# Layer 1's q and k projections by seven block products instead of eight, on one core of Trainium2

## The chip, the cores and the metric

The kernel runs on one core of one Trainium2 chip. The core has five engines with queues of their own: TensorE (PE, matmuls; its weight loads are shown as PEld), VectorE (DVE), ScalarE (ACT), GpSimd (POOL) and SyncE (SP, which here issues the transfers). [...] The metric is the device time of one execution in microseconds, as a median over runs.

## The reference

The input x has the shape 1 x 128 x 256 x 256: 128 rows of 256 tokens with 256 channels. There are two layers, both in float32, and each adds its result to its input.

```python
x = x + _L0_conv_ref(_gn(x), ...)   # gated attention along a row, 8 heads, pair bias from z
x = x + _L1_conv_ref(_gn(x), w_in, b_in, w_out, b_out, 16)

def _L1_conv_ref(x, w_in, b_in, w_out, b_out, band):     # H = 4 heads, D = 64
    qkv = x2 @ w_in.T + b_in
    q, k, v = jnp.split(qkv, 3, axis=-1)
    ...
    scores = jnp.einsum('bhid,bhjd->bhij', q, k) / jnp.sqrt(D)
    keep = jnp.abs(i - j) <= band
    scores = jnp.where(keep, scores, -jnp.inf)
    attn = jax.nn.softmax(scores, axis=-1)
    out = jnp.einsum('bhij,bhjd->bhid', attn, v)
    y = out @ w_out.T + b_out
```

`_gn` is a group normalization over the whole picture with 32 groups of 8 channels. The change concerns layer 1 alone, and of it the products that give q and k.

## The kernel before, in words

A first stage reads x and z and takes the statistics of the first normalization. Layer 0 follows, and writes its result to DRAM. Then comes layer 1, in `fast_kernel` from line 1665 on. (A second version, `general_kernel`, runs only if a check at the end asks for it.)

Layer 1 works on pairs of rows, 64 of them, each an object of the class `Pair1`. The data of a pair lie transposed: channels on the partitions, in KC = 2 chunks of 128, and the two rows' 512 tokens along the free axis. The steps of a pair are methods:

- `turn`: VectorE transposes the loaded rows (`xs`) to `xT`. `centre(k)`: ScalarE subtracts the mean from chunk k (`xgT`), and after the second chunk GpSimd adds the output bias to the copy `xt` that waits for the residual. The scale of the normalization is multiplied into `w_in` once, in `norm1`.
- `project(which, m)`: TensorE makes one 128-channel chunk m of q or k for both rows, by two matmuls of 128x128 weights with 512 columns (line 1745). ScalarE copies it out with its bias (line 1749). A pair needs four such calls, eight matmuls.
- `values(r)`: four matmuls of 256 columns make v of row r (line 1760), and ScalarE copies them out (line 1764).
- `scores(r)`: small matmuls over the band's blocks (line 1774), the exponential on ScalarE (line 1782), and the band's mask on GpSimd (line 1784).
- `apply(r)`: small matmuls give the weighted values (`o_eo`) and the sums of the weights (`su_eo`), even and odd blocks in tiles of their own (line 1802).
- `combine(r)`: ScalarE copies the odd halves (lines 1812 and 1813), VectorE adds the even ones, takes the reciprocal (line 1815) and makes `oT` (lines 1814 to 1818).
- `out_row(r)`: four matmuls with `w_out` (line 1833), VectorE adds the residual (line 1837), and SP sends the pair to the output.

The main loop (line 1886) is written under `tc.manual_schedule()`: every engine gets its instructions in the order in which the program text issues them, and each engine runs its queue in that order. The tile layer adds the semaphore waits that the tiles' uses call for. A turn of the loop works on several pairs at once: it scores and applies the rows of `now`, finishes `was`, projects `nxt`, and centres `nn`:

```python
now.scores(0); was.apply(1); was.out_row(0); was.combine(1)
nxt.project("qT", 0); nxt.project("kT", 0); nxt.project("qT", 1); nn.centre(0)
now.scores(1); now.apply(0); now.combine(0); nxt.project("kT", 1)
nxt.values(0); nxt.values(1); was.out_row(1); nn.centre(1); n3.turn()
```

PSUM, the memory that matmuls write to, has eight banks of 512 float32 columns. Layer 1 divides them so: two tiles of one bank for products (`ps1_mm`, used in turn by `project`, `values` and `out_row` through `mm1`), one tile of two banks for the scores (`ps1_s`), and four tiles of one bank each for `o_eo` and `su_eo`.

Of the kernel before, what the change touches and what calls it, by code (L numbers as in the profile page):

```python
# [9 lines left out]
F32 = mybir.dt.float32  # L10
AF = mybir.ActivationFunctionType
ALU = mybir.AluOpType
# [4 lines left out]
P = 128  # L17
# [756 lines left out]
def fast_kernel(  # L774
# [889 lines left out]
    rsum1 = dram.tile([NP, H1, 2, I], F32, name="rsum1")  # L1664
    with tc.tile_pool(name="l1", bufs=2) as sb, tc.tile_pool(
        name="l1s", bufs=4
    ) as sm, tc.tile_pool(name="ps1_mm", bufs=2, space=PSUM) as ps_mm, tc.tile_pool(
        name="ps1_s", bufs=1, space=PSUM
    ) as ps_s, tc.tile_pool(name="ps1_o", bufs=1, space=PSUM) as ps_o:

        def mm1(name):
            return ps_mm.tile([P, 512], F32, name=name, tag="mm")

        nM1 = const.tile([P, KC], F32, name="nM1")

        def norm1():
# [4 lines left out]
            ps = ps_s.tile([P, 2, 512], F32, name="ps_gn", tag="s")  # L1681
# [14 lines left out]
            nc.vector.tensor_scalar_add(R1c, ps[:, 1, 2:4], 1e-5)  # L1696
            nc.gpsimd.tensor_tensor(R1c, R1c, mhalf[:, :KC], ALU.pow)
            nc.vector.tensor_scalar_mul(nM1, ps[:, 1, 0:2], -1.0)
            for n in range(3):
                for k in range(KC):  # L1700
                    at = slice(n * C, (n + 1) * C)
                    nc.vector.tensor_scalar_mul(w_in[:, k, at], w_in[:, k, at], R1c[:, k : k + 1])


        o_eo = [ps_o.tile([P, 2, I], F32, name=f"ps_o1_{n}", tag=f"o{n}") for n in range(2)]
        su_eo = [ps_o.tile([P, I], F32, name=f"ps_su1_{n}", tag=f"su{n}") for n in range(2)]
        for n in range(2):
            nc.vector.memset(o_eo[n], 0.0)
            nc.vector.memset(su_eo[n], 0.0)

        class Pair1:

# [19 lines left out]
            def centre(self, k):  # L1732
# [3 lines left out]
                if k == KC - 1:  # L1736
                    nc.gpsimd.tensor_tensor(self.xt, self.xt, bcast(bout_r, 1, 2 * NB), ALU.add)

            def project(self, which, m):
# [3 lines left out]
                ps = mm1("ps_p1")  # L1743
                for k in range(KC):
                    nc.tensor.matmul(  # L1745
                        ps, w_in[:, k, n * C + m * P : n * C + (m + 1) * P], self.xgT[:, k, :],
                        start=(k == 0), stop=(k == KC - 1),
                    )
                nc.scalar.activation(
                    getattr(self, which)[:, m, :], ps, AF.Identity, bias=bin_c[:, n * KC + m : n * KC + m + 1]  # L1750
                )

            def values(self, r):
                if r == 0:
                    self.v = sb.tile([P, 2, NB, C], F32, name="v1", tag="v")
                ps = mm1("ps_v1")
                for b in range(NB):
                    t = r * NB + b
                    for k in range(KC):
                        nc.tensor.matmul(  # L1760
                            ps[:, b * C : (b + 1) * C], self.xgT[:, k, t * P : (t + 1) * P], w_in[:, k, 2 * C : 3 * C],
                            start=(k == 0), stop=(k == KC - 1),
                        )
                nc.scalar.copy(self.v[:, r, :, :].rearrange("p b c -> p (b c)"), ps)

            def scores(self, r):

                ps = ps_s.tile([P, 2, 512], F32, name="ps_sc1", tag="s")
                at = lambda q, c, j: ps[:, q, (c * 2 + j) * W : (c * 2 + j + 1) * W]
                for c in range(KC):  # L1770
                    for k in range(NK):
# [32 lines left out]
                                )  # L1804

            def combine(self, r):

                if r == 0:
                    self.rv = sb.tile([P, 2, I], F32, name="rv1", tag="rv", bufs=3)
                rv = self.rv  # L1810
                odd = sm.tile([P, 3, I], F32, name="odd1", tag="odd", bufs=2)
                nc.scalar.copy(odd[:, 2, :], su_eo[1])
                nc.scalar.copy(odd[:, :2, :], o_eo[1])
                nc.vector.tensor_tensor(odd[:, 2, :], su_eo[0], odd[:, 2, :], ALU.add)
                nc.vector.reciprocal(rv[:, r, :], odd[:, 2, :])  # L1815
                nc.vector.tensor_tensor(odd[:, :2, :], o_eo[0], odd[:, :2, :], ALU.add)
                oT = sb.tile([P, 2, I], F32, name="oT1", tag="oT", bufs=3)
                nc.vector.tensor_tensor(oT, odd[:, :2, :], bcast(rv[:, r, :], 1, 2), ALU.mult)  # L1818
                self.oT[r] = oT
                if r == 1 and self.p < NP - LATE:  # L1820
                    nc.sync.dma_start(rsum1[self.p].rearrange("q r i -> q (r i)"), rv[0:P:DH].rearrange("q r i -> q (r i)"))
                elif r == 1 and self.p < NP - 1:
                    check(rv.rearrange("p r i -> p (r i)"), 1e-16, 1e8, sm)
                elif self.p == NP - 1:
                    check(rv[:, r, :], 1e-16, 1e8, sm)

            def out_row(self, r):
                if r == 0:
                    self.yo = sb.tile([P, 2 * NB, C], F32, name="yo", tag="yo")
                ps = mm1("ps_y1")  # L1830
                for b in range(NB):
                    for k in range(KC):
                        nc.tensor.matmul(  # L1833
                            ps[:, b * C : (b + 1) * C], self.oT[r][:, k, b * P : (b + 1) * P], w_out[:, k, :],
                            start=(k == 0), stop=(k == KC - 1),
                        )
                nc.vector.tensor_tensor(  # L1837
                    self.yo[:, r * NB : (r + 1) * NB, :], ps.rearrange("p (b c) -> p b c", b=NB),
                    self.xt[:, r * NB : (r + 1) * NB, :], ALU.add,
                )  # L1840
                s0 = 2 * self.p
# [22 lines left out]
        with tc.manual_schedule():  # L1864
            now, nxt = pair1(0), pair1(1)
            now.turn()
            nxt.turn()
            norm1()
            for k in range(KC):
                now.centre(k)  # L1870
            for m in range(KC):
                now.project("qT", m)
                now.project("kT", m)
            for r in range(2):
                now.values(r)
            for k in range(KC):
                nxt.centre(k)
        check_all(eb.rearrange("p h b i -> p (h b i)"), math.exp(-20.0), math.exp(20.0))
        mask_t = sb.tile([S, I], F32, name="mask_all", bufs=1)
        nc.sync.dma_start(mask_t, mask)  # L1880
# [3 lines left out]
        with tc.manual_schedule():  # L1884
            was = Nobody()
            for p in range(NP - 1):
# [6 lines left out]

                now.scores(0)
                was.apply(1)
                was.out_row(0)
                was.combine(1)
                nxt.project("qT", 0)
                nxt.project("kT", 0)
                nxt.project("qT", 1)  # L1900
                nn.centre(0)

                now.scores(1)
                now.apply(0)
                now.combine(0)
                nxt.project("kT", 1)
                if p < NP - 2:
                    nxt.values(0)
                    nxt.values(1)
                was.out_row(1)  # L1910
                nn.centre(1)
                n3.turn()
                if checks and p > 0:
                    checks.pop(0)()
# [20 lines left out]
        ps = mm1("ok_ps")  # L1935
        nc.tensor.matmul(ps[:, 0:1], ones, tot, start=True, stop=True)
        nc.vector.tensor_scalar(verdict, ps[0:1, 0:1], P - 0.5, None, ALU.is_lt)


@with_exitstack  # L1940
# [62 lines left out]
```

## Time and profile before

| | us |
|---|---|
| Median of three runs | 3310.61 |
| Lowest and highest | 3309.5, 3310.71 |
| The profiled execution, its own time | 3316.03 |
| Its span, first to last instruction | 3314.3 |
| Layer 1 in it: first scores to the end of the last row's addition (line 1837) | 2133.2 to 3307.8 |

The profile is of one execution. Its page gives, by engine, the busy time and the share of the span; the span in 40 slices with the busy share in tenths and TensorE's granted clock in tenths of full speed; and the chain of work that ended last, followed back from the end. The timeline lists an engine's instructions, merged where equal ones follow each other: start, duration, engine, line, operation, output and input tiles, shapes, count, and in brackets how long the engine was idle before and what ended the wait. A float32 matmul appears as two records, and their recorded durations overlap, so that the time of one is read from start to start.

### The profile page before, as it was taken

The page shows a single profiled execution, that of the slowest core. Times are in us where ns is not written, and L with a number is a line of the kernel's source. Part 1 is how long each engine was busy: PE and PEld are TensorE (multiplying, and loading weights), DVE is VectorE, ACT ScalarE, POOL GpSimd, SP SyncE. Part 2 cuts the span into 40 slices and gives each one's busy share as a digit, 9 for nine tenths or more (in the row PEclk, how much of TensorE's full clock was granted, in tenths as well). Part 3 has the DMA queues.
Part 4 walks back from the last instruction along what each step waited for, and adds up shares of the span by engine and source line. Part 5 has one row for each costly group of instructions (what it writes and reads, how often), then busy time and mean ns, then how long its engine had stood idle before and what let it go on. Part 6 is the DMA issues. An engine that isn't in the chain of part 4 may idle for free.

```text
span 3314.3 us, 80768 instructions
## 1 busy us (share of the span) xinstructions
PE 3157.9 (95%) x34656; PEld 1977.2 (60%) x34656; DVE 2121.6 (64%) x3179; ACT 1452.7 (44%) x2121; POOL 1962.8 (59%) x1375
## 2 busy tenths in 40 slices
PE   5389999999999999999999999699999999999998
PEld 3255555555555555555555555466666666666666
DVE  7955666666666666666666666466655555555566
ACT  2264444444444444444444444244444444444443
POOL 2378777777787777787887776233333333333332
PEclk8699999999999999999999999899999999999999
DMA  9951212212221222222122211533333434343431
GB/s 354 375 137 43 75 49 75 75 46 65 72 75 49 75 75 60 64 64 69 49 75 75 75 49 52 104 79 91 85 90 86 92 85 91 85 92 84 92 90 54
DMA packets 464879, 295.92 MB, mean 89 GB/s; under 512 B 312480, under 2 KB 413728, under 8 KB 463360
## 3 DMA queue, kind: packets, MB, share of 16 engines
q1 hardware_dynamic: 459440, 287.76, 31.7%
q8 instruction: 275, 4.51, 0.6%
q10 hardware_dynamic: 5072, 2.90, 0.3%
q14 instruction: 92, 0.75, 0.1%
HBM read 221.85 MB, written 68.75 MB: 88 GB/s over the span
## 4 chain that ended last, share of the span: by engine, by line
PE 91%; DVE 3%; DMA 3%; ACT 1%; POOL 1%; SPq 1%; issue 0%; ACTq 0%; POOLq 0%; DVEq 0%
PE ps_p L1296 21%; PE ps_p L1745 14%; PE ps_sc L1330 8%; PE ps_y L1833 7%; PE ps_ov L1362 7%; PE ps_v L1760 7%; PE ps_y L1417 7%; PE ps_v L1311 6%; PE ps_o L1802 3%; PE ps_su L1370 3%; PE ps_sc L1774 3%; PE ps_x L1274 2%; PE ps_su L1802 1%; DVE st L1178 1%; DVE zst L1103 1%; DMA zt<-in_z_dram 1%
## 5 line engine op out<-in xcount | busy, mean ns | idle before, releaser
L1351 POOL TENSOR_TENSOR eboth<-e 128x512 f32<-128x512 f32 x512 | 640.6, 1273 | 392.9 <-DVE e L1346 389.7
L1346 DVE TENSOR_TENSOR e<-ps_sc,eb 128x1024 f32<-128x1024 f32 x512 | 603.1, 1219 | 307.0 <-ACT ps_sc L1337 306.9
L1337 ACT ACTIVATE ps_sc<-ps_sc 128x1024 f32<-128x1024 f32 x512 | 492.8, 1006 | 509.2 <-PE ps_sc L1330 509.2
L1784 POOL TENSOR_TENSOR e<-e,bw 128x384 f32<-128x384 f32 x256 | 259.5, 1035 | 769.8 <-ACT e L1782 769.8
L1745 PE MATMUL ps_p<-xgT,w_in 128*128 128x512 f32 x1024 | 470.3, 602 | 4.5 <-issue 3.7
L1745 PEld LDWEIGHTS ps_p<-xgT,w_in 128*128 128x128 f32 x1024 | 190.1, 191 | 203.7 <-issue 174.8
L1330 PE MATMUL ps_sc<-qT,kT 32*128 32x256 f32 x4096 | 293.3, 400 | 2.1 <-ACT kT L1300 2.1
L1296 PE MATMUL ps_p<-xnT,wq 128*128 128x512 f32 x512 | 267.3, 634 | 3.5 <-POOL xnT L1283 3.1
L1833 PE MATMUL ps_y<-w_out,oT 128*128 128x256 f32 x1024 | 250.3, 388 | 2.6 <-DVE oT L1818 2.6
L1837 DVE TENSOR_TENSOR yo<-ps_y,xt 128x512 f32<-128x512 f32 x128 | 88.4, 690 | 251.9 <-PE ps_y L1833 149.7
L1362 PE MATMUL ps_ov<-e,v 128*32 128x256 f32 x4096 | 247.7, 382 | 0.0
L1417 PE MATMUL ps_y<-wo,oT 128*128 128x256 f32 x1024 | 242.1, 379 | 2.0 <-POOL oT L1407 1.2
L1417 PEld LDWEIGHTS ps_y<-wo,oT 128*128 128x128 f32 x1024 | 194.3, 190 | 82.5 <-issue 59.3
L1311 PE MATMUL ps_v<-wv,xnT 128*128 128x256 f32 x1024 | 242.2, 379 | 0.0
L1330 PEld LDWEIGHTS ps_sc<-qT,kT 32*128 32x128 f32 x4096 | 184.9, 184 | 94.4 <-issue 83.6
L1296 PE MATMUL ps_p<-xnT,wk 128*128 128x512 f32 x512 | 240.8, 592 | 0.0
L1296 PE MATMUL ps_p<-xgT,wg 128*128 128x512 f32 x512 | 236.8, 605 | 0.0
L1760 PE MATMUL ps_v<-w_in,xgT 128*128 128x256 f32 x1024 | 231.8, 379 | 0.0
L1815 DVE RECIPROCAL rv<-odd 128x256 f32<-128x256 f32 x128 | 224.4, 1753 | 4.4
L1760 PEld LDWEIGHTS ps_v<-w_in,xgT 128*128 128x128 f32 x1024 | 194.4, 190 | 53.5 <-issue 30.1
L1317 DVE TENSOR_TENSOR v<-ps_v,vb_r 128x512 f32<-128x512 f32 x128 | 88.6, 692 | 206.8 <-PE ps_v L1311 206.8
L1311 PEld LDWEIGHTS ps_v<-wv,xnT 128*128 128x128 f32 x1024 | 189.6, 190 | 50.8 <-issue 31.0
(169 smaller groups left out, 4989.9 us busy)
## 6 DMA issues: line engine op xcount, KB each, us to landing
xa<-in_x_dram SPq DMA_DIRECT2D x8, 4096.0 KB
xt<-in_x_dram SPq DMA_DIRECT2D x64, 512.0 KB
x<-xo SPq DMA_DIRECT2D x16, 2048.0 KB
xs<-x SPq DMA_DIRECT2D x256, 128.0 KB
xt<-x SPq DMA_DIRECT2D x64, 512.0 KB
rvb<-rsum SPq DMA_DIRECT2D x252, 128.0 KB
out_dram<-yo SPq DMA_DIRECT2D x63, 512.0 KB
zt<-in_z_dram SPq DMA_DIRECT2D x15, 2048.0 KB
```

The source lines that it names most:

```text
L1296: nc.tensor.matmul(ps, w[:, k, m * P : (m + 1) * P], getattr(self, src)[:, k, :], start=(k == 0), stop=(k == KC - 1),)
L1311: nc.tensor.matmul(self.ps_v[:, b * C : (b + 1) * C], self.xnT[:, k, t * P : (t + 1) * P], wv[:, k, :], start=(k == 0), stop=(k == KC - 1),)
L1330: nc.tensor.matmul(self.pss[q // 2][:, q % 2, b, :], self.kT[rs, c, r * I + b * P : r * I + (b + 1) * P], self.qT[rs, c, r * I : (r + 1) * I],
L1337: nc.scalar.activation(self.pss[a], self.pss[a], AF.Exp)
L1346: nc.vector.tensor_tensor(e, pss[a], eb[:, h : h + 2], ALU.mult)
L1351: nc.gpsimd.tensor_tensor(t, es[a][:, :, 0, :], es[a][:, :, 1, :], ALU.add)
L1362: nc.tensor.matmul(ov[q * D0 : (q + 1) * D0, c, :], self.v[:, r, b, h * D0 : (h + 1) * D0], es[q // 2][:, q % 2, b, :], start=(b == 0), st ...
L1417: nc.tensor.matmul(self.ps_y[:, b * C : (b + 1) * C], self.oT[r][:, k, b * P : (b + 1) * P], wo[:, k, :], start=(k == 0), stop=(k == KC - 1),)
L1745: nc.tensor.matmul(ps, w_in[:, k, n * C + m * P : n * C + (m + 1) * P], self.xgT[:, k, :], start=(k == 0), stop=(k == KC - 1),)
L1760: nc.tensor.matmul(ps[:, b * C : (b + 1) * C], self.xgT[:, k, t * P : (t + 1) * P], w_in[:, k, 2 * C : 3 * C], start=(k == 0), stop=(k == ...
L1784: nc.gpsimd.tensor_tensor(e[:, q], e[:, q], bcast(bw.rearrange("p b w -> p (b w)"), 1, KC), ALU.mult)
L1833: nc.tensor.matmul(ps[:, b * C : (b + 1) * C], self.oT[r][:, k, b * P : (b + 1) * P], w_out[:, k, :], start=(k == 0), stop=(k == KC - 1),)
```

## The change

Of a pair's centred data take the four blocks b[k][r] (chunk k, row r; 128x256), and of the q weights the four blocks w(m, k) of 128x128; the same for k. Strassen's form (in Winograd's arrangement) makes the four output blocks from seven products instead of eight. Its parts:

- `mix_weights`, once: four sums and differences of weight blocks on GpSimd (`wst`).
- `differences`, per pair: four differences of data blocks on GpSimd (`dT`), issued after the pair's second `centre`.
- `product(n, i)`: one matmul of 256 columns, for q (n = 0) or k (n = 1). A product goes to block x or block y of a tile of two banks; x lies in the first and y in the second. Products 1, 6, 7 and 4 go to x one after the other, each added to what is there, and ScalarE copies x out with the bias after each of them: the first three to `u`, the last to the result. Product 2 goes to y, later 5, and 3 is added to 5.
- `join(n, i)`: VectorE adds y and one part of `u` to a block of the result, after products 2, 5 and 3.

PSUM is laid out anew: one ring of two tiles of two banks each (`two1`), which the scores, the products of q, the products of k, and the values share in turn. Both rows' values lie in one such tile. The tile `su_y` of two banks holds the sums of `apply` in one half of each bank and the product of `out_row` in the other.

The turn of the loop is written anew as well: `combine` is split in three, `out_row(0)` moves behind the products 7 and the old pair's `weigh`, and all products stand in the first half of the turn.

```diff
-    ) as sm, tc.tile_pool(name="ps1_mm", bufs=2, space=PSUM) as ps_mm, tc.tile_pool(
-        name="ps1_s", bufs=1, space=PSUM
-    ) as ps_s, tc.tile_pool(name="ps1_o", bufs=1, space=PSUM) as ps_o:
+    ) as sm, tc.tile_pool(name="ps1_s", bufs=2, space=PSUM) as ps_s, tc.tile_pool(
+        name="ps1_o", bufs=1, space=PSUM
+    ) as ps_o:
...
+        def two1(name):
+            return ps_s.tile([P, 2, 512], F32, name=name, tag="s")
...
-        su_eo = [ps_o.tile([P, I], F32, name=f"ps_su1_{n}", tag=f"su{n}") for n in range(2)]
+        su_y = ps_o.tile([P, 2, 2, I], F32, name="ps_su_y1", tag="su")
+        su_eo = [su_y[:, n, 0] for n in range(2)]
...
+            def differences(self):
+                self.dT = sb.tile([P, 4, I], F32, name="dT1", tag="dT")
+                b = [[self.xgT[:, k, r * I : (r + 1) * I] for r in range(2)] for k in range(KC)]
+                t1, t2, t3, t4 = (self.dT[:, n] for n in range(4))
+                nc.gpsimd.tensor_tensor(t1, b[0][1], b[0][0], ALU.subtract)
+                nc.gpsimd.tensor_tensor(t2, b[1][1], t1, ALU.subtract)
+                nc.gpsimd.tensor_tensor(t3, b[1][1], b[0][1], ALU.subtract)
+                nc.gpsimd.tensor_tensor(t4, b[1][0], t2, ALU.subtract)
...
+            def product(self, n, i):
+                if len(self.ps) == n:
+                    self.ps.append(two1("ps_qk"))
+                x, y = self.ps[n][:, 0, :I], self.ps[n][:, 1, :I]
+                w = lambda m, k: w_in[:, k, n * C + m * P : n * C + (m + 1) * P]
+                b = lambda k, r: self.xgT[:, k, r * I : (r + 1) * I]
+                to, lhs, rhs, start = {
+                    1: (x, w(0, 0), b(0, 0), True),
+                    2: (y, w(0, 1), b(1, 0), True),
+                    6: (x, wst[:, 1, n], self.dT[:, 1], False),
+                    5: (y, wst[:, 0, n], self.dT[:, 0], True),
+                    7: (x, wst[:, 2, n], self.dT[:, 2], False),
+                    4: (x, w(1, 1), self.dT[:, 3], False),
+                    3: (y, wst[:, 3, n], b(1, 1), False),
+                }[i]
+                nc.tensor.matmul(to, lhs, rhs, start=start, stop=True, skip_group_check=True)
+                bias = lambda m: bin_c[:, n * KC + m : n * KC + m + 1]
+                u = self.u[n]
+                if i in (1, 6, 7):
+                    at = (1, 6, 7).index(i)
+                    nc.scalar.activation(u[:, at], x, AF.Identity, bias=bias(at // 2))
+                elif i == 4:
+                    nc.scalar.activation(self.to[n][:, 1, 0:I], x, AF.Identity, bias=bias(1))
+
+            def join(self, n, i):
+                m, r, at = {2: (0, 0, 0), 5: (1, 1, 2), 3: (0, 1, 1)}[i]
+                nc.vector.tensor_tensor(
+                    self.to[n][:, m, r * I : (r + 1) * I], self.ps[n][:, 1, :I], self.u[n][:, at], ALU.add
+                )
...
             def values(self, r):
                 if r == 0:
                     self.v = sb.tile([P, 2, NB, C], F32, name="v1", tag="v")
-                ps = mm1("ps_v1")
+                    self.ps_v = two1("ps_v1")
+                ps = self.ps_v[:, r]
...
             def out_row(self, r):
-                ps = mm1("ps_y1")
+                ps = su_y[:, :, 1]
...
                 now.scores(0)
                 was.apply(1)
+                nxt.begin_fast()
+                nxt.product(0, 1)
+                was.copy_odd(1)
+                nxt.product(1, 1)
+                for n in range(2):
+                    nxt.product(n, 2)
+                    nxt.join(n, 2)
+                was.invert(1)
+                for i in (6, 5, 7):
+                    for n in range(2):
+                        nxt.product(n, i)
+                for n in range(2):
+                    nxt.join(n, 5)
+                was.weigh(1)
                 was.out_row(0)
-                was.combine(1)
-                nxt.project("qT", 0)
-                nxt.project("kT", 0)
-                nxt.project("qT", 1)
+                for n in range(2):
+                    nxt.product(n, 4)
+                    nxt.product(n, 3)
+                    nxt.join(n, 3)
                 nn.centre(0)
 
                 now.scores(1)
                 now.apply(0)
                 now.combine(0)
-                nxt.project("kT", 1)
                 if p < NP - 2:
                     nxt.values(0)
                     nxt.values(1)
                 was.out_row(1)
                 nn.centre(1)
+                nn.differences()
                 n3.turn()
```

The first pair is still projected by `project`, ahead of the loop. `copy_odd`, `invert` and `weigh` hold the lines of the old `combine`: ScalarE's two copies; the sum and the reciprocal; the weighting and what follows it.

More of the change, by code (lines that the diff above doesn't have):

```diff
@@ L1666, in fast_kernel @@
         name="l1s", bufs=4
-    ) as sm, tc.tile_pool(name="ps1_mm", bufs=2, space=PSUM) as ps_mm, tc.tile_pool(
-        name="ps1_s", bufs=1, space=PSUM
-    ) as ps_s, tc.tile_pool(name="ps1_o", bufs=1, space=PSUM) as ps_o:
-        def mm1(name):
-            return ps_mm.tile([P, 512], F32, name=name, tag="mm")
+    ) as sm, tc.tile_pool(name="ps1_s", bufs=2, space=PSUM) as ps_s, tc.tile_pool(
[3 more added lines that the diff above has]
+            return ps_s.tile([P, 2, 512], F32, name=name, tag="s")
         nM1 = const.tile([P, KC], F32, name="nM1")
+        wst = sb.tile([P, 4, 2, P], F32, name="wst", bufs=1)
         def norm1():
@@ L1680, in norm1 @@
             R1c = sm.tile([P, KC], F32, name="gn_R", bufs=1)
-            ps = ps_s.tile([P, 2, 512], F32, name="ps_gn", tag="s")
+            ps = two1("ps_gn")
             by_group = lambda a: a.rearrange("p (g e) -> p g e", e=GE)
@@ L1702, in norm1, with mix_weights @@
                     nc.vector.tensor_scalar_mul(w_in[:, k, at], w_in[:, k, at], R1c[:, k : k + 1])
+        def mix_weights():
+            a = [[w_in[:, k, 0 : 2 * C].rearrange("p (n m c) -> p m n c", n=2, m=KC)[:, m] for k in range(KC)]
+                 for m in range(KC)]
+            s1, s2, s3, s4 = (wst[:, n] for n in range(4))
+            nc.gpsimd.tensor_tensor(s1, a[1][0], a[1][1], ALU.add)
+            nc.gpsimd.tensor_tensor(s2, s1, a[0][0], ALU.subtract)
+            nc.gpsimd.tensor_tensor(s3, a[0][0], a[1][0], ALU.subtract)
+            nc.gpsimd.tensor_tensor(s4, a[0][1], s2, ALU.subtract)
         o_eo = [ps_o.tile([P, 2, I], F32, name=f"ps_o1_{n}", tag=f"o{n}") for n in range(2)]
-        su_eo = [ps_o.tile([P, I], F32, name=f"ps_su1_{n}", tag=f"su{n}") for n in range(2)]
+        su_y = ps_o.tile([P, 2, 2, I], F32, name="ps_su_y1", tag="su")
+        su_eo = [su_y[:, n, 0] for n in range(2)]
         for n in range(2):
             nc.vector.memset(o_eo[n], 0.0)
-            nc.vector.memset(su_eo[n], 0.0)
+        nc.vector.memset(su_y, 0.0)
         class Pair1:
@@ new lines, in begin_fast @@
+            def begin_fast(self):
+                self.ps, self.to, self.u = [], [], []
+                for which in ("qT", "kT"):
+                    to = sb.tile([P, KC, N2], F32, name=f"{which}1", tag=which)
+                    setattr(self, which, to)
+                    self.to.append(to)
+                    self.u.append(sm.tile([P, 3, I], F32, name="u1", tag=f"u{which}", bufs=2))
+            def product(self, n, i):
[21 more added lines that the diff above has]
+                    nc.scalar.activation(self.to[n][:, 1, 0:I], x, AF.Identity, bias=bias(1))
@@ L1742, in project @@
                     setattr(self, which, sb.tile([P, KC, N2], F32, name=f"{which}1", tag=which))
-                ps = mm1("ps_p1")
+                ps = two1("ps_p1")[:, 0]
                 for k in range(KC):
@@ L1766, in scores @@
             def scores(self, r):
-                ps = ps_s.tile([P, 2, 512], F32, name="ps_sc1", tag="s")
+                ps = two1("ps_sc1")
                 at = lambda q, c, j: ps[:, q, (c * 2 + j) * W : (c * 2 + j + 1) * W]
@@ L1806, in combine, with copy_odd, invert, weigh @@
             def combine(self, r):
+                self.copy_odd(r)
+                self.invert(r)
+                self.weigh(r)
+            def copy_odd(self, r):
                 if r == 0:
                     self.rv = sb.tile([P, 2, I], F32, name="rv1", tag="rv", bufs=3)
-                rv = self.rv
-                odd = sm.tile([P, 3, I], F32, name="odd1", tag="odd", bufs=2)
+                odd = self.odd = sm.tile([P, 3, I], F32, name="odd1", tag="odd", bufs=2)
                 nc.scalar.copy(odd[:, 2, :], su_eo[1])
                 nc.scalar.copy(odd[:, :2, :], o_eo[1])
+            def invert(self, r):
+                odd = self.odd
                 nc.vector.tensor_tensor(odd[:, 2, :], su_eo[0], odd[:, 2, :], ALU.add)
-                nc.vector.reciprocal(rv[:, r, :], odd[:, 2, :])
+                nc.vector.reciprocal(self.rv[:, r, :], odd[:, 2, :])
+            def weigh(self, r):
+                rv, odd = self.rv, self.odd
                 nc.vector.tensor_tensor(odd[:, :2, :], o_eo[0], odd[:, :2, :], ALU.add)
@@ L1833, in out_row @@
                         nc.tensor.matmul(
-                            ps[:, b * C : (b + 1) * C], self.oT[r][:, k, b * P : (b + 1) * P], w_out[:, k, :],
+                            ps[:, b], self.oT[r][:, k, b * P : (b + 1) * P], w_out[:, k, :],
                             start=(k == 0), stop=(k == KC - 1),
@@ L1837, in out_row @@
                 nc.vector.tensor_tensor(
-                    self.yo[:, r * NB : (r + 1) * NB, :], ps.rearrange("p (b c) -> p b c", b=NB),
+                    self.yo[:, r * NB : (r + 1) * NB, :], ps,
                     self.xt[:, r * NB : (r + 1) * NB, :], ALU.add,
@@ L1870, in fast_kernel @@
                 now.centre(k)
+            mix_weights()
             for m in range(KC):
@@ L1877, in fast_kernel @@
                 nxt.centre(k)
+            nxt.differences()
         check_all(eb.rearrange("p h b i -> p (h b i)"), math.exp(-20.0), math.exp(20.0))
@@ L1934, in fast_kernel @@
         nc.vector.tensor_reduce(tot, ok[:, : len(done)], AX.X, ALU.min)
-        ps = mm1("ok_ps")
-        nc.tensor.matmul(ps[:, 0:1], ones, tot, start=True, stop=True)
-        nc.vector.tensor_scalar(verdict, ps[0:1, 0:1], P - 0.5, None, ALU.is_lt)
+        ps = two1("ok_ps")
+        nc.tensor.matmul(ps[:, 0, 0:1], ones, tot, start=True, stop=True)
+        nc.vector.tensor_scalar(verdict, ps[0:1, 0, 0:1], P - 0.5, None, ALU.is_lt)
 @with_exitstack
```

## The prediction

> **What bounds the kernel now.** I read the page's busy table first, then its slices, the chain that ended last, and then the timeline of one turn of layer 1's main loop, engine by engine.
>
> ```profile
> PE 3157.9 (95%) x34656; PEld 1977.2 (60%) x34656; DVE 2121.6 (64%) x3179; ACT 1452.7 (44%) x2121; POOL 1962.8 (59%) x1375
> PE   5389999999999999999999999699999999999998
> PEclk8699999999999999999999999899999999999999
> PE 91%; DVE 3%; DMA 3%; ACT 1%; POOL 1%; SPq 1%; issue 0%; ACTq 0%; POOLq 0%; DVEq 0%
> ```
>
> TensorE carries the end: 91% of the chain. Layer 1 fills the slices after the one marked 6. Its waits end nowhere on TensorE, and the clock is full. So whatever makes TensorE wait there is paid in full. The stretch table for 100 us in its middle gives the slack of the others: DVE 55, ACT 46, POOL 34 us.
>
> ```profile
> 2400.00:2500.00 100.00, 100.00 (x1677) 70.06 (x1676) 55.35 (x60) 45.92 (x77) 34.50 (x28) 1.00 0.37 86
> ```
>
> One half of a turn, TensorE's timeline and then ScalarE's (start, duration, engine, line):
>
> ```profile
> 2710.50 1.98 PE L1745 MATMUL ps_p<-xgT,w_in 128*128 128x512 f32 x4
> 2712.32 3.62 PE L1760 MATMUL ps_v<-w_in,xgT 128*128 128x256 f32 x16
> 2715.78 1.89 PE L1833 MATMUL ps_y<-w_out,oT 128*128 128x256 f32 x8
> 2717.60 0.89 PE L1774 MATMUL ps_sc<-qT,kT 64*64 64x96 f32 x32
> ...
> 2714.25 0.59 ACT L1764 COPY v<-ps_v 128x512 f32<-128x512 f32 x1 [1.04 <-PE ps_v L1760]
> 2715.98 0.59 ACT L1764 COPY v<-ps_v 128x512 f32<-128x512 f32 x1 [1.14 <-PE ps_v L1760]
> ```
>
> A float32 matmul is two records, so x16 is eight matmuls of 256 columns. Start to start they take 2715.78 - 2712.32 = 3.46 us, **0.4325 us each**. The projections of this turn take 2703.15 to 2708.39 and 2710.50 to 2712.32, 7.06 us for eight of 512 columns, 0.88 each: time goes with columns, and halving a matmul costs nothing. The next turn's scores start 18.40 us after this one's (2699.2 to 2717.60). The first value copy starts at 2714.25 while its four matmuls gave way to the next at 2714.05: **0.20 us** from the end of a stream to the start of its reader. TensorE does not notice that copy, because the second half of the values goes to another buffer.
>
> The reverse way, from a reader to TensorE, shows once in layer 1, at its start:
>
> ```profile
> 2133.80 1.33 ACT L1735 ACTIVATE xgT<-xT,nM 128x512 f32<-128x512 f32 x2
> 2134.57 0.30 PEld L1745 LDWEIGHTS ps_p<-xgT,w_in 128*128 128x128 f32 x2 [0.66 <-ACT xgT L1735]
> 2134.58 1.98 PE L1745 MATMUL ps_p<-xgT,w_in 128*128 128x512 f32 x4 [0.47 <-ACT xgT L1735]
> ```
>
> The first of the two copies ends at 2134.52; the weight load starts 0.05 later. In the single records the second half of that matmul starts 0.53 us after the first, where a running stream has 0.43: the load was not ahead, 0.11 more. So **0.16 us** from a reader's end to a stream.
>
> [...] The blocks x and y of a product tile lie in different banks[...]. [...] in the tail, after 2.55 us without work, the eight records of an output row take 3.65 us instead of 1.89. [...]
>
> **The change part by part.** *Saved:* fourteen matmuls of 256 columns, 14 x 0.4325 = 6.06 us, for 7.06: **1.00 us** a turn.
>
> *Added waits.* The lists of the built programs show what the diff doesn't: the order is kept by whole tile. A product into y waits for ScalarE's copy out of x of the same tile, and a product into x for VectorE's join out of y. The two halves of the values now share a tile, and the second waits for the copy of the first. A copy of 128x256 with bias has no row. The plain copies are 0.372 us (256 columns) and 0.592 (512), the biased one 0.688 (512); I take 0.688 - 0.22 = 0.47, with bounds 0.372 and 0.688. A join is like the sum at L1814, 0.42. So a full round trip through ScalarE is 0.20 + 0.47 + 0.16 = 0.83, through VectorE 0.78.
>
> Let the first product of q (q1) end at 0; k1 ends at 0.43.
> - q2 waits for q1's copy: 0.83. Stall 0.40. Ends 1.26.
> - k2 waits for k1's copy. ScalarE has two copies of the old row's sums between (start to start 0.38 + 0.27 + 0.50): it starts at 0.20 + 1.15 = 1.35, ends 1.82, k2 can go at 1.98. Stall 0.72. Ends 2.41.
> - q6 waits for q2's join: 1.26 + 0.78 = 2.04, passed. Ends 2.84. k6 waits for k2's join: 3.19. Stall 0.35. Ends 3.62.
> - q5 waits for q6's copy: 3.67. Stall 0.05. Ends 4.10. k5 waits for k6's copy: 4.45. Stall 0.35. Ends 4.88.
> - q7, k7 and the output row run to 7.48 without a wait; q4 needs q5's join, which follows q7's copy (5.31 + 0.67) and the reciprocal (1.75 us, from about 3.4): done at 6.5.
> - q3 waits for q4's copy, just issued: stall 0.83. k3 for k4's: 0.83.
> - Second half of the values: 0.20 + 0.586 + 0.16 = 0.95.
>
> Sum 0.40 + 0.72 + 0.35 + 0.05 + 0.35 + 0.83 + 0.83 + 0.95 = **4.48 us** a turn.
>
> *Costed at nothing:* six joins (2.5 us, VectorE goes from 10 to 13 of about 22 us). They stand behind the row addition, the transpose and, in some turns, a check (0.39 + 1.38 + 0.69): these end about 4.2 us into a turn, 0.2 after q2's join could start (q1 ends 2.5 into it), and q6 still has its join in time. Eight biased ScalarE copies of 256 columns for four of 512 (3.8 us for 2.75): idle time of that engine, but for the stalls counted above. Four differences on GpSimd, an estimated 0.72 us each (between 1.00 at 384 columns and half of 1.27 at 512): done some 2 us into the turn, before the masks of the next scores and q6. The later output row hands VectorE its addition later; scores of the second half need q3's join, which is done at about 9.8 while k3 ends at 10.9. That cover is gone in the last six turns, where a check of the reciprocals (0.42 + 0.69 + 0.69) stands before it: some 0.2 us each. The sums and the output row share a tile now, so ScalarE's copies of the sums wait for the row addition before: done 0.9 us into the turn, 2 us before the copies can start. The weight mixes run once on GpSimd, beside the first projections. No DMA is added or moved past another on SP.
>
> *Sum:* 4.48 - 1.00 = +3.48 a turn, 62 turns with values = +216; the 63rd without, +2.5; the prologue's values +1; the checks +1: **+221 us**. The profiled execution had a span of 3314.3 and took 3316.0, 5.4 above the median of 3310.6. Against it the sum is 3537; against the median **3532**.
>
> **Rivals.**
> *Waits that cost nothing (faster).* q and k are interleaved so that one product of the other always covers a wait. If every release came in time, 63 x 1.00 is gained: **3247**. The point is 1.00 us of stall a turn. Against it: one product covers 0.43 us, a round trip is 0.8, and q3, k3 and the values have nothing between. The values' 0.95 alone eats the gain, and it is made of measured rows.
> *The wait is cheaper than a round trip.* If the biased copy takes 0.372 (0.5 us less a turn over the chain above) and the weight load is ahead after all (0.11 less on seven waits): 2.2 us a turn, **3450**.
> *The clock falls.* [...] A tenth of the 17.4 us of work at half rate is +1.7 us a turn on top: **3640**. The tail speaks for it; against it, its idle stretch was 2.55 us, and no stall here is over 1 us.
> *Nothing changes:* the products and waits are in the built program, and TensorE has no idle time to take them; excluded.
>
> **How the numbers follow.** What a measurement of this kernel can tell from no change is about 0.2%, 7 us. The chain as worked: 0.76, cheaper waits 0.12, clock 0.09, hidden waits 0.02, a near draw 0.01. The chain's own bounds are half of the cheap case below (-40) and 0.8 us a turn above, if each wait has another 0.1 us (+50): 3490 to 3582. Towards the cheaper and slower cases I go to 3480 and 3590. All but the last two cases are slower: 0.97.
>
> **What would show it.** In the after profile: TensorE idle some 20% of each turn in layer 1, in the list of waits under ScalarE's copies of u, of qT and kT (0.83 each) and of v (0.95 each), and under k's join; turns of 21.9 us; busy time of the projections lower by about 1 us a turn; layer 0 and the clock as before. Wrong if the turns are under 20 us, if the waits name VectorE's queue or GpSimd in the main, or if the clock leaves 1.0 inside layer 1.

## The result, and the profile after

The changed kernel takes 3547.59 us (median of four runs, 3545.17 to 3550.01), the kernel before 3310.66 beside it (3309.5 to 3315.72): 236.9 us more, a ratio of 1.0713 with a 95% interval of 1.0694 to 1.0731. The profiled spans are 3543.4 and 3314.3. Layer 1, from its first projection to the end of the span, takes 1428.4 us in place of 1195.3 (+233.1); what stands ahead of it happened to be 4.0 us shorter in this execution.

The page of the changed kernel: busy time by engine, the slices of TensorE and of its clock, and the shares of the chain that ended last.

```profile
PE 3226.7 (91%) x35412; PEld 2080.0 (59%) x35412; DVE 2264.0 (64%) x3556; ACT 1508.6 (43%) x2373; POOL 2167.5 (61%) x1631
PE   5389999999999999999999968888888888888887
PEclk9699999999999999999999989999999999999999
PE 84%; ACT 7%; DVE 4%; DMA 2%; issue 2%; POOL 0%; ACTq 0%; POOLq 0%; DVEq 0%; SPq 0%
```

In the slices the 9s of layer 1 have become 8s, and layer 0 is as it was. The clock is full until the last two output rows. In the chain ScalarE has gone from 1% to 7% and VectorE from 3% to 4%: work that used to lie beside TensorE now lies on the path. The stretch table for the same 100 us as before (busy time and instructions of PE, PEld, DVE, ACT, POOL, then clock, share of DMA and GB/s) says the same of one stretch: TensorE's 100.00 has become 88.06, and no other engine is near full.

```profile
2400.00:2500.00 100.00, 88.06 (x1425) 64.50 (x1423) 60.37 (x83) 42.13 (x81) 44.77 (x41) 1.00 0.29 65
```

One turn on TensorE, from its timeline (start, duration, then in brackets the idle time before and what ended it):

```profile
2802.08 1.99 PE L1822 MATMUL ps_v<-w_in,xgT 128*128 128x256 f32 x8
2804.75 1.99 PE L1822 MATMUL ps_v<-w_in,xgT 128*128 128x256 f32 x8 [0.68 <-ACT v L1826]
...
2812.91 0.70 PE L1785 MATMUL ps_qk<-xgT,w_in 128*128 128x256 f32 x2 [0.43 <-ACT u L1790]
2813.44 3.51 PE L1785 MATMUL ps_qk<-dT,wst 128*128 128x256 f32 x12
...
2819.67 0.70 PE L1785 MATMUL ps_qk<-xgT,wst 128*128 128x256 f32 x2 [0.56 <-ACT qT L1792]
2820.20 0.59 PE L1785 MATMUL ps_qk<-dT,w_in 128*128 128x256 f32 x2
2821.36 0.70 PE L1785 MATMUL ps_qk<-xgT,wst 128*128 128x256 f32 x2 [0.56 <-ACT kT L1792]
2821.99 0.89 PE L1836 MATMUL ps_sc<-qT,kT 64*64 64x96 f32 x32
```

Where the kernel before had two rows of values in one stream of sixteen records, there are two streams of eight with a hole between them. Products 3 of q and k stand alone, each behind a hole. The brackets understate the holes, as do the lists of waits, which add the brackets up, since a record's duration runs beyond the start of the next one: between 2818.51 (product 4 of q) and 2819.67 (product 3 of q) lie 1.16 us where a running stream has 0.43, and the second record of product 3 comes another 0.10 late: 0.83 in all. ScalarE's timeline shows the copies that they wait for:

```profile
2804.11 0.58 ACT L1826 COPY v<-ps_v 128x512 f32<-128x512 f32 x1 [1.06 <-PE ps_v L1822]
...
2819.14 0.47 ACT L1792 ACTIVATE qT<-ps_qk,bin_c 128x256 f32<-128x256 f32 x1 [1.69 <-PE ps_qk L1785]
```

The list of waits of the whole span (us in total, times, longest), first under TensorE's matmuls, then under its weight loads, names the same few buffers in all turns. 63 times product 3 waits for a copy that has nothing to do with its own block y:

```profile
PE ps_v L1822 <- ACT v L1826: 42.1, 63, 0.7
PE ps_qk L1785 <- ACT qT L1792: 35.6, 63, 0.6
PE ps_qk L1785 <- ACT kT L1792: 35.6, 63, 0.6
PE ps_qk L1785 <- ACT u L1790: 26.4, 62, 0.4
...
PEld ps_qk L1785 <- ACT u L1790: 127.1, 251, 0.8
PEld ps_qk L1785 <- DVE kT L1796: 30.6, 63, 0.5
```

In single records, start to start, the turn takes **22.03 us** against 18.39, and 61 of the 63 turns are alike. The steps that exceed a running stream's are the stalls, eight in each turn:

| stall of TensorE | predicted, us | measured, us |
|---|---|---|
| product 2 of q, for ScalarE's copy of 1 | 0.40 | 0.40 |
| product 2 of k, the same | 0.72 | 0.69 |
| product 6 of k, for VectorE's join of 2 | 0.35 | 0.35 |
| product 5 of q, for the copy of 6 | 0.05 | 0.05 |
| product 5 of k, the same | 0.35 | 0.35 |
| product 3 of q, for the copy of 4 | 0.83 | 0.83 |
| product 3 of k, the same | 0.83 | 0.83 |
| values of the second row, for the copy of the first | 0.95 | 0.94 |
| sum | 4.48 | 4.44 |

### The profile page after: what moved, and what is told of

It is laid out like the page before. It is cut to its first block, busy times and chain, and to the rows that moved or that the text cites. A ratio compares the mean times of both kernels' runs of the same rounds, so it can differ in the third digit from the quotient of the medians.

```text
span 3543.4 us, 83104 instructions
## 1 busy us (share of the span) xinstructions
PE 3226.7 (91%) x35412; PEld 2080.0 (59%) x35412; DVE 2264.0 (64%) x3556; ACT 1508.6 (43%) x2373; POOL 2167.5 (61%) x1631
## 4 chain that ended last, share of the span: by engine, by line
PE 84%; ACT 7%; DVE 4%; DMA 2%; issue 2%; POOL 0%; ACTq 0%; POOLq 0%; DVEq 0%; SPq 0%
PE ps_p L1296 20%; PE ps_qk L1785 11%; PE ps_sc L1330 8%; PE ps_v L1822 7%; PE ps_ov L1362 7%; PE ps_su_y L1904 6%; PE ps_v L1311 6%; PE ps_y L1417 6%; PE ps_o L1864 3%; PE ps_su L1370 3%; PE ps_sc L1836 3%; ACT u L1790 2%; PE ps_x L1274 2%; PE ps_su_y L1864 1%; DVE st L1178 1%
## 5 line engine op out<-in xcount | busy, mean ns | idle before, releaser
L1822 PE MATMUL ps_v<-w_in,xgT 128*128 128x256 f32 x1024 | 255.1, 392 | 42.1 <-ACT v L1826 42.1
L1790 ACT ACTIVATE u<-ps_qk,bin_c 128x256 f32<-128x256 f32 x378 | 177.8, 478 | 235.8 <-PE ps_qk L1785 235.8
L1904 PE MATMUL ps_su_y<-w_out,oT 128*128 128x256 f32 x1024 | 245.9, 384 | 3.8 <-DVE odd L1882 2.8
L1822 PEld LDWEIGHTS ps_v<-w_in,xgT 128*128 128x128 f32 x1024 | 184.1, 189 | 96.7 <-ACT v L1826 67.1
L1785 PE MATMUL ps_qk<-dT,wst 128*128 128x256 f32 x756 | 210.2, 400 | 10.7
L1904 PEld LDWEIGHTS ps_su_y<-w_out,oT 128*128 128x128 f32 x1024 | 196.4, 192 | 32.3 <-DVE odd L1882 3.6
```

The costliest lines, as they stand in the source:

```text
L1785: nc.tensor.matmul(to, lhs, rhs, start=start, stop=True, skip_group_check=True)
L1822: nc.tensor.matmul(ps[:, b * C : (b + 1) * C], self.xgT[:, k, t * P : (t + 1) * P], w_in[:, k, 2 * C : 3 * C], start=(k == 0), stop=(k == ...
L1904: nc.tensor.matmul(ps[:, b], self.oT[r][:, k, b * P : (b + 1) * P], w_out[:, k, :], start=(k == 0), stop=(k == KC - 1),)
```

## The experiments

**Theory:** the tile is the unit by which uses are ordered. Products write y while ScalarE reads x, in different banks, but the two are one tile, so each write waits for a round trip: from the end of a stream to its reader, the reader's own time, and back to the next stream. **Rivals:** small matmuls cost more than their columns say; or the added work of GpSimd, VectorE and ScalarE costs the time, whatever is waited for. A run for which no range is given is one execution; it is read by its turns, most of which repeat to 0.02 us, before its total.

### The values in tiles of their own

```diff
-                    self.ps_v = two1("ps_v1")
-                ps = self.ps_v[:, r]
+                ps = two1("ps_v1")[:, 0]
```

> The changed kernel, but each row's values take a tile of the ring of their own. Waits theory (the loss is TensorE standing at waits that whole-tile order adds): the second half of the values no longer waits for the first one's copy, 0.95 us less in each of 62 turns, turn 21.1 us, total about 3488. Work theory (the loss is the added joins, copies and differences): nothing changes, about 3547. Small-product theory (256-column products cost more in their place than 0.43 us): 3547.

Measured: 3487.61 us, a turn of 21.09, so 0.94 less. The list of waits of TensorE's matmuls from 2200 to 3250 us has no ps_v left:

```profile
PE ps_qk L1785 <- ACT kT L1792: 28.3, 50, 0.6
PE ps_qk L1785 <- ACT qT L1792: 28.3, 50, 0.6
PE ps_qk L1785 <- ACT u L1790: 21.0, 49, 0.4
```

The wait of the second row is priced, and is all that this part of the layout costs.

### Products 4 of q and k first, then 3

```diff
                 was.out_row(0)
+                for i in (4, 3):
+                    for n in range(2):
+                        nxt.product(n, i)
                 for n in range(2):
-                    nxt.product(n, 4)
-                    nxt.product(n, 3)
                     nxt.join(n, 3)
```

> The changed kernel, but products 4 of q and of k come first and then products 3 of both. Waits theory: q3 waits 0.40 instead of 0.83 us, since k4 lies between, and k3 not at all: 1.26 us less in each of 63 turns, turn 20.8, total about 3468. Work theory: the same work, 3547. Small-product theory: the same products, 3547.

Measured: 3488.82 us, 21 us more than expected, 7 of them ahead of layer 1; a turn of 20.91, 1.12 less where 1.26 was expected. Product 3 of k does not wait any more and that of q waits 0.40, as expected, but the next scores now wait 0.16 for the join of 3. And at the end, where five turns take 22.03 us, TensorE and VectorE (lines of two timelines) show this:

```profile
3382.80 0.89 PE L1836 MATMUL ps_sc<-qT,kT 64*64 64x96 f32 x32 [1.20 <-DVE qT L1796]
...
3380.40 0.69 DVE L959 SCALAR_TENSOR_TENSOR chk<-rv,chk 128x512 f32<-128x512 f32 x1
3381.13 0.69 DVE L960 TENSOR_REDUCE ok<-chk 128x1 f32<-128x512 f32 x1
3381.73 0.68 DVE L1908 TENSOR_TENSOR yo<-ps_su_y,xt 128x512 f32<-128x512 f32 x1
3382.33 0.41 DVE L1796 TENSOR_TENSOR qT<-ps_qk,u 128x256 f32<-128x256 f32 x1
```

Here the check of the reciprocals stands before the joins in VectorE's queue, and with product 3 of q earlier, the scores wait 1.2 us for it. In the changed kernel the same check was covered by the stall of product 3 of k (its turns there take 22.04): a wait that is removed takes its cover with it.

### The kernel before, with its matmuls halved

```diff
-                for k in range(KC):
-                    nc.tensor.matmul(ps, ..., self.xgT[:, k, :], ...)
+                for r in range(2):
+                    for k in range(KC):
+                        nc.tensor.matmul(ps[:, r * I : (r + 1) * I], ..., self.xgT[:, k, r * I : (r + 1) * I], ...)
```

> The kernel before, with each projection matmul of 512 columns cut into two of 256: sixteen weight loads a pair instead of eight. Small-product theory: each 256-column matmul costs clearly more than half of a 512-column one, 3400 and more. Waits theory and work theory: 16 x 0.4325 = 6.92 us for 7.06, no difference that can be told, 3305 to 3318.

Measured: 3323.79 us, above the expected range, and 9 us more than the run of the kernel before beside it; but the turn is 18.43 (18.39), and layer 1 takes 1198.5 us (1195.3). Against the profiled span of before (+7.8), 4.6 us lie ahead of layer 1, which starts at 2123.6 in place of 2119.0; that start lay between 2115.0 and 2123.6 over all runs here. Sixteen matmuls of 256 columns cost what eight of 512 do, to 0.04 us a turn: this rival falls.

### The layout without the products

```diff
-                nxt.begin_fast()
-                ... products 1 to 7 and their joins ...
+                was.combine(1)
+                for m in range(KC):
+                    nxt.project("qT", m)
+                    nxt.project("kT", m)
                 was.out_row(0)
```

The ring, `su_y` and GpSimd's four differences stay; q and k are made by `project`, as before.

> The changed kernel with its PSUM ring, its shared sum and output tile, and its differences on GpSimd, but with the four projections in place of the products and joins. Waits theory: of the added waits only the values' remains, turn 18.39 + 1.0 = 19.4, total about 3373. Work theory: the differences on GpSimd cost part of the loss, the joins the rest; a total of 3400 or more would speak for it. Small-product theory: near the kernel before, 3311.

Measured: 3378.77 us, a turn of 19.34, 0.95 over the kernel before. The list of waits, from 2200 to 3250 us, has one entry for TensorE's matmuls:

```profile
PE ps_v L1822 <- ACT v L1826: 37.2, 55, 0.7
```

So the differences, this order and the shared `su_y` cost nothing in a turn; the values' shared tile is the whole price of the layout there. The rest of the loss comes with the products. This run lacks the joins and the added copies of ScalarE, so it excludes added work for GpSimd alone; the run with x and y as separate tiles, below, has as many joins and is faster than the kernel before.

### Three covers together

To the two edits of the first experiments, one is added: `was.copy_odd(1)` goes behind product 1 of k, so that ScalarE copies product 1 of k before the old row's sums.

```diff
                 nxt.product(0, 1)
-                was.copy_odd(1)
                 nxt.product(1, 1)
+                was.copy_odd(1)
```

> The changed kernel with its tiles for q and k as they are, but with the values in tiles of their own, products 4 of both before products 3 of both, and k1's copy ahead of the old row's sums on ScalarE. Waits theory: the two first give what they gave alone (0.94 and 1.12 us a turn), and k2's wait of 0.69 goes while q6 waits 0.35 for its join: together 2.4 us less, turn 19.6, about 3400. It stays slower than the kernel before, since a round trip of 0.8 us stands against one product of 0.43. Work theory: 3547.

Measured: 3390.57 us, a turn of 19.35 in most of the loop (19.58 in many of the first fifteen, 20.5 to 20.7 in five of the last, where the checks stand before a join). What is left is 0.40 to 0.42 at products 2, 6, 5 and 3 of q and 0.16 at the scores, 1.78 us together. That is one product's cover (0.43) against a round trip (0.83), each time. These orders do not bring it under the 0.83 that the products save.

### Sums in pieces as cover

Products of q and k side by side in one bank (the next section shows the code), and `apply` cut in two, so that its small matmuls cover the waits of products 2 and 6; the output row is cut in two as well:

```diff
+                was.apply(1, (0, 1))
+                nxt.products(2)
+                was.apply(1, (2,))
+                was.copy_odd(1)
+                nxt.join(2)
+                nxt.products(6)
```

> Products side by side as in the kernel with two tiles, but with the small matmuls of the old row cut in three and laid between the levels as cover, the output row cut in two, and the checks left where they were. Waits theory: the two waits are covered but for 0.1 and 0.1, against that two more changes between small and large matmuls (some 0.2 us each) and 0.6 us in 14 turns and 2.4 in 6 where a check stands before a join: about 3290. Work theory: 3400 and more.

Measured: 3313.89 us, 24 us over what was expected and the same as the kernel before. The turns take 18.23 to 18.3 us, and 19.6 in most of the last six, where the checks stand before a join. Of the 0.83 us that the products save, 0.14 goes to one wait that is left, before product 4. The other 0.53 goes with two more changes from large matmuls to small ones and back, dearer than the 0.2 us each that was expected.

### Side by side, with x and y as separate tiles

x of q and of k share one bank, y of both another, each a tile of its own; ScalarE copies both x at once, the joins add the bias; each row of values has its own tile.

```diff
+            def products(self, i):
+                if i == 1:
+                    self.px = mm1("ps_x1")
+                elif i == 2:
+                    self.py = mm1("ps_y1")
+                ps = self.px if i in (1, 6, 7, 4) else self.py
...
+                    nc.tensor.matmul(ps[:, n * I : (n + 1) * I], lhs, rhs, ...)
+                if i in (1, 6, 7):
+                    at = (1, 6, 7).index(i)
+                    nc.scalar.copy(self.u[:, at].rearrange("p n i -> p (n i)"), ps)
...
+                nxt.products(1)
+                was.copy_odd(1)
+                nxt.products(2)
+                nxt.join(2)
+                was.invert(1)
+                for i in (6, 5, 7):
+                    nxt.products(i)
+                ... the old row's output, join 5, weigh ...
+                nxt.products(4)
+                nxt.products(3)
+                nxt.join(3)
+                ... the checks ...
```

> The same seven products, but product i of q and product i of k lie side by side in one bank: x and y are two tiles of one bank each, each level is copied by one ScalarE copy of 512 columns without bias, and the joins add the bias. The values again have a tile for each row, the scores a tile of their own; the order is 1, 2, 6, 5, 7, output row, 4, 3 for both at once, and the checks on VectorE stand behind the last join. Waits theory: product 2 waits for nothing, 6 for the copy of 1 (0.95 us, 0.87 of it covered by product 2 of both: 0.1), 5 for the join of 2 (0.2), 7, 4 and 3 for nothing; saving 1.0 less 0.1 for two slow starts, so a turn of 17.7 to 17.8 us and about 3270, faster than the kernel before. Work theory: as many joins and differences as in the changed kernel, slower than before, 3400 and more.

Measured: **3295.96 us** (five runs, 3294.34 to 3299.67), a ratio to the kernel before of 0.9949 with an interval of 0.9936 to 0.9963. It is 0.5% faster than the kernel before, and layer 1 takes 1175.5 us. The turn is 18.01: 0.83 saved and 0.44 given back, 0.14 at product 6 (the copy of 1) and 0.30 at product 5 (the join of 2). TensorE's timeline has products 2, 6 and 5 of one turn:

```profile
2814.95 1.03 PE L1791 MATMUL ps_y<-xgT,w_in 128*128 128x256 f32 x4
2815.88 1.10 PE L1791 MATMUL ps_x<-dT,wst 128*128 128x256 f32 x4
2817.02 1.13 PE L1791 MATMUL ps_y<-dT,wst 128*128 128x256 f32 x4
```

From start to start these are 0.93 and 1.14 us, where a running pair has 0.86; the second record of the pair that waited comes a little later too.

The expected turn was 17.7 to 17.8 and the expected time 3270; 0.17 us of the turn's excess is the saving, which was again taken as 1.00. The page of this run has the slices of TensorE back at 9:

```profile
PE 3131.2 (95%) x35412; PEld 2109.1 (64%) x35412; DVE 2262.4 (69%) x3556; ACT 1444.0 (44%) x2184; POOL 2159.1 (66%) x1631
PE   5389999999999999999999999699999999999998
```

### The same, with x and y in one tile

```diff
-                    self.px = mm1("ps_x1")
-                elif i == 2:
-                    self.py = mm1("ps_y1")
+                    self.pxy = mm2("ps_xy1")
+                    self.px, self.py = self.pxy[:, 0], self.pxy[:, 1]
```

The values' two rows are paired in one tile as well. Instructions, their order and the banks' number are those of the run above.

> The kernel with products side by side, same order and same instructions, with one difference: the two banks for x and y are one tile, and so are the two for the values. Waits theory: product 2 waits for the copy of 1 (0.95), 6 for the join of 2 (1.12), 5 for the copy of 6 (0.95), 3 for the copies of 4 (1.2), the second values for the first one's copy (0.95); 4.9 us more in a turn than with two tiles, 22.6 us, about 3575. Work theory: no difference between the two.

Measured: 3677.2 us, 381 more than with separate tiles, by the grouping of banks into tiles alone. The list of waits from 2200 to 3250 us:

```profile
PE ps_xy L1798 <- ACT u L1804: 59.4, 88, 0.7
PE ps_xy L1798 <- DVE kT L1815: 49.7, 44, 1.1
PE ps_xy L1798 <- ACT kT L1807: 40.9, 44, 0.9
PE ps_v L1841 <- ACT v L1845: 29.7, 44, 0.7
```

With separate tiles this list was empty. Turns take 23.15 and 24.65 us alternately. The shorter ones are 5.14 us longer than with separate tiles; 62 of these would give some 3615, and the rest was not expected. They had been expected at 22.6. The longer ones have a second cause, which the timeline of TensorE shows:

```profile
2720.28 1.10 PE L1798 MATMUL ps_xy<-dT,wst 128*128 128x256 f32 x4 [1.13 <-DVE kT L1815]
2722.05 3.43 PE L1798 MATMUL ps_xy<-dT,wst 128*128 128x256 f32 x8 [0.68 <-ACT u L1804]
```

Eight records take 3.43 us, where they take 1.89 to 1.99 elsewhere. In single records they step by 0.427 us in place of 0.216 for about 3.4 us, once in 47.8 us, which is every second turn; the trace's record of the granted clock has 0.5 for 3.41 us at each of these places. This is the clock falling, the rival that the prediction gave 3640: it is real, but the changed kernel stays short of it.

### More cover for the side-by-side products

```diff
                 was.apply(1)
+                was.copy_odd(1)
+                was.sum_odd(1)
                 nxt.products(1)
-                was.copy_odd(1)
                 nxt.products(2)
+                was.out_half(0, 0)
                 nxt.join(2)
                 was.invert(1)
                 for i in (6, 5, 7):
                     nxt.products(i)
-                for b in range(NB):
-                    was.out_half(0, b)
+                was.out_half(0, 1)
```

> Side by side products as in j3_side_by_side, with half of the output row between products 2 and 6 and the other half between 7 and 4; ScalarE's copies of the old sums and VectorE's sum of the odd halves stand ahead of product 1's copy, so that the shared tile su_y is free before that half row writes to it, and the reciprocal stands behind the join of 2. Waits theory: in j3 product 6 stalled 0.14 us (for the copy of 1) and product 5 0.30 us (for the join of 2) a turn. With 0.86 us of output row between, the copy of 1 and the join of 2 are both done before their successors' turn: the turn falls from 18.01 to 17.57 us, which is the turn of the kernel before (18.39) less the whole saving of 0.83, and the time to 3296 - 62 x 0.44 = 3269. Rival: the chain through VectorE (sum of the odd halves, joins, reciprocal 1.75 us) now runs late and the join of 5 holds product 3 instead; then the turn stays at about 18.0 and the time at about 3296.

Measured: 3294.25 us (five runs, 3293.46 to 3300.79), ratio 0.9944, interval 0.993 to 0.9957: which cannot be told apart from the run with separate tiles, and is 25 us over what was expected. Products 6 and 5 wait no more, but 7 and 4 do, 0.14 each: one pair of products or half an output row is 0.86 us of cover, and ScalarE's 512-column copy with its way there and back needs about 1.00. The turn is 17.85, not 17.57. And two turns near the end take 22.16 and 20.74 us. VectorE's timeline of the second, then the output row behind each on TensorE:

```profile
3196.36 1.53 DVE L959 SCALAR_TENSOR_TENSOR chk<-rv,chk 128x512 f32<-128x512 f32 x1
...
3199.04 2.59 DVE L959 SCALAR_TENSOR_TENSOR chk<-sums,chk 128x384 f32<-128x384 f32 x1
3201.66 0.55 DVE L960 TENSOR_REDUCE ok<-chk 128x1 f32<-128x384 f32 x1
3202.13 0.41 DVE L1896 TENSOR_TENSOR odd<-ps_su_y,odd 128x256 f32<-128x256 f32 x1
...
3180.50 3.36 PE L1922 MATMUL ps_su_y<-w_out,oT 128*128 128x256 f32 x8 [2.68 <-DVE odd L1896]
3202.60 1.99 PE L1922 MATMUL ps_su_y<-w_out,oT 128*128 128x256 f32 x8 [2.35 <-DVE odd L1896]
```

The two steps of the checks (the first and third line) took 0.69 (nothing of GpSimd beside it) and 1.24 (beside its masks) in the changed kernel; here the first runs beside GpSimd's masks and the second mostly beside its addition to `xt`, and the output row behind them waits 2.68 us in the first of these turns and 2.35 in the second. In the first the clock then halves for 3.41 us, and the row takes 3.36 in place of 1.99. Of the 62 x 0.16 = 10 us that the turns gain, 7 are given back there.

## Why the prediction was right, and where it was off

*The direction and the mechanism* held. The stalls came as worked, one by one (4.44 for 4.48), from two measured ends of a round trip and the durations of rows. The biased copy took 0.47 to 0.478, the value taken between the bounds; the GpSimd differences 0.72 to 0.74 (0.72 estimated), but for the first of each pair, most of which took 1.17 to 1.18. The pair of runs with x and y apart and together shows the cause: the grouping into tiles. Smaller matmuls are excluded by the run that halves them, GpSimd's added work by the run without the products, and the joins by the run with separate tiles, which has them all and is faster than the kernel before.

*The saving of 1.00 us a turn* is the term that was mis-sized: it is **0.83**. The 7.06 us read for eight projections held two changes of group. A running 512-column matmul takes 0.859, eight of them 6.87; fourteen of 256 columns at 0.4316 take 6.04. The rest of the 7.06 is the first record after the small matmuls of `apply`, which steps 0.320 in place of 0.216 (0.104 more), and the step into the scores, 0.309 in place of 0.216 (0.093 more). Both stay, whichever matmuls stand there. The halved matmuls, whose turn is 18.43, bear it out. Over 62 turns this is 10.5 us.

*The sum.* A turn costs 4.44 - 0.83 = 3.61 more, and was measured at 3.64 (18.39 to 22.03). From the first projection to the second turn layer 1 takes 4.2 us more, the next 61 turns 221.7, the last turn 3.7 and what follows 3.5: together the 233.1 measured. The prediction had 221.

*The end of the kernel* was not in the sum. The shared `su_y` makes an output row wait 0.92 us for VectorE's sum of the odd halves in the last turn, which was put at +2.5. Behind the loop, output rows wait 0.92 and 0.94 for such a sum and 0.99 for a row's addition, and `apply`'s sums wait 1.36 for an addition. Two output rows run at half clock there, where the kernel before has one. With what the kernel before already waited there taken off, the end costs 3.5.

*The first turn* has two waits that neither the others nor the kernel before have. Product 1 of k waits for the exponential, since it takes the tile of the ring that the scores had, and product 4 of q waits for the join of 5, since no output row stands between:

```profile
2131.35 1.96 PE L1785 MATMUL ps_qk<-xgT,w_in 128*128 128x256 f32 x6 [0.61 <-ACT e L1844]
...
2137.34 0.67 PE L1785 MATMUL ps_qk<-dT,w_in 128*128 128x256 f32 x2 [0.68 <-DVE qT L1796]
```

*What was costed at nothing* cost nothing in an ordinary turn: the joins, the ScalarE copies, the differences and the new place of the output row. The eight stalls account for the turn to 0.03 us, and the run without the products shows it for GpSimd and `su_y`. The checks of the last six turns were put at 0.2 us each and cost 0.01.

*The rivals.* Hidden waits: not so, and by how much a single product falls short is shown by three covers together. Cheaper waits: the biased copy and the weight load were as dear as taken. The clock: 1.0 in all turns of the changed kernel. The worst 3.41 us of its turns hold 1.77 us without a stream, 2.12 in the first turn; those before a halved stretch in the run with one tile held 1.94 to 2.20.

## What to carry to other kernels

Before blocks are given to a tile, ask what each engine does to it while another still reads: a tile that two engines take turns in costs a round trip each time that nothing covers it, here 0.8 to 1.0 us, even where the blocks lie in different banks. Price a saving of matmuls from single records inside a running stream; a stretch from first to last holds changes of shape that stay. And when a wait is taken away, look at what it covered: the next wait stands right behind it.

## What the runs showed of the hardware

**The clock fell on part-idle stretches.** In the records of the granted clock of the kernel before and of the changed one, every stretch at 0.5 lasts 3.41 us or a multiple of it, up to 30.7 us, but for the one that the end cuts off. In the run with one tile, the 3.41 us ahead of a halved stretch of the loop held 1.94 to 2.20 us without a stream (the time by which the steps from record to record exceed 0.216), mostly in two stalls of which the longest was 1.29, and the matmuls ran for the rest. The changed kernel, with at most 1.77 us by the same count in any such length of its turns, and 2.12 in the first, kept its clock in all. In the last run a wait of 2.68 us was followed by a halved stretch and one of 2.35 was not. So neither the sum of the stalls nor the longest of them tells alone when the clock falls, and what sets it off no run here shows.

**A change of shape costs TensorE.** The first large record after packed small ones (64x96) takes 0.104 us more, and the first small group after large ones starts 0.093 later, in the kernel before and in the changed one alike. These two are not the whole price of cutting a group of small matmuls: in the run with sums in pieces, two more changes there and back went with 0.53 us a turn.

**VectorE beside GpSimd.** In the changed kernel the weighting (`oT` from `odd` and `rv`, 128x512) took 0.69 us in the 66 executions of 128 that had no GpSimd operation beside them, and 1.24 to 1.34 in the 62 that had; the reciprocal took 1.75 in both cases. In the last run the first step of the check took 1.53 us beside GpSimd's mask, for 0.69 without, and the two masks took 2.40 for the 1.95 in the run with separate tiles. What makes both slower beside each other, no run here shows.

**Tiles of a bank.** The two runs that differ in tiles alone put a price on ordering uses by a tile of two banks in place of two tiles of one: 381 us, the fallen clock included.
